# Row-wise self products on one core: new first blocks, shorter waits on GpSimd, and fifteen small loads behind the last store

## The chip, the core and the metric

The kernel runs on one core of a Trainium2 chip. The metric is the device time of one execution, in microseconds, as a median over runs. Products are made on VectorE (DVE), ScalarE (ACT) and GpSimd (POOL); SyncE (SP) issues the stores and GpSimd most of the loads; 16 DMA engines move the data. TensorE only counts the first stores.

## The reference

For each of 4096 rows of 256 floats, all products of two entries of the row with i <= j, in the order of the upper triangle:

```
dot = jnp.einsum('bi,bj->bij', inputs, inputs)      # inputs: (4096, 256) float32
iu, ju = jnp.triu_indices(256)
return dot[:, iu, ju]                               # (4096, 32896) float32
```

The input has 4.2 MB and the output 539 MB.

## The kernel before

The input lies in SBUF as one tile `x`: each of the 128 partitions holds 32 rows, in 16 groups of two (`REPEAT`), so one group is 256 rows of the output. The 32896 columns of a group are cut at multiples of 64 into three *pieces* (`PIECES`) of 10944, 10944 or 11008 columns. A piece of 128 x 2 rows fills one of two places, `o0` and `o1`, and leaves as one store of about 11 MB. Within a piece the work is a list of *runs* (`runs`): for one i, the products x[i] * x[j] for consecutive j. One VectorE or GpSimd instruction does a run for both rows of a group (two runs at once at some places), one ScalarE activation does a run for one row.

The loop (`all_pieces`) runs over `passes` = 8 times two groups, each time over `PASS` = 6 pieces. In it `tail` gives the last runs of a piece, up to a budget of 19.4 us by its cost function, to VectorE, and the others to GpSimd (`blocks`, with `ahead` false). VectorE reads one operand from `xv`, a copy of the current group in SBUF, and the other from `xp`, a copy in PSUM; GpSimd reads both from `xv`. `interleave` and `schedule` order the instructions so that one which writes one element into the next run's place is followed by that run a few instructions later, with a wait between them. Before a piece VectorE waits until the place's earlier store has landed (`free`) and passes that on through `go`, which GpSimd waits for (line 330). When GpSimd is done with a piece it waits for its own counter `g_own` and raises `g_done` (line 348). SP (`sync`) waits for `v_done` and `g_done` and issues the store of the piece.

The first two pieces (`ahead` true) are made differently. The first is cut at `FIRST` into six blocks that are stored one by one, so that the stores begin early; `split` divides the runs of a block between ScalarE (first runs) and VectorE (the rest), by cost functions in nanoseconds. In its first block VectorE reads both operands from `x`; then it copies `x` to `xp` in PSUM (line 232), takes GpSimd's `x_copied` (line 239) and goes on with `xv` and `xp`. In the second piece (`HELPED`) GpSimd does the last runs, up to 15 us, after `go`.

SP issues three loads at the start (`NEAR`; the first brings the first group), the rest of `x` comes from GpSimd: ten loads (`EARLY`, nine of which take every ninth partition, 14 each) with a small load, `mark`, between them, and further loads in the third turn of the loop (`LATE`). A `mark` brings two short runs of `MARK` floats to each of some partitions of a tile `marks` that nothing reads; the number of its partitions, with that of the loads, sets which DMA engines the next load uses. Right after the first load of these GpSimd waits for the first group and copies it to `xv` (lines 417 to 419).

At the end SP takes the counters of the loads and, last, `free` of both places (lines 427 to 431): the kernel ends when the last store has landed.

Of the kernel before, what the change touches and what calls it, by code (L numbers as in the profile page):

```python
# [8 lines left out]
F32 = mybir.dt.float32  # L9
# [3 lines left out]
P = 128  # L13
UNIT = 64
REPEAT = 2
# [9 lines left out]
COMB = 9  # L25
FORE, AFT = 5, 14
TENS, FIVES, SKIP = 100, 25, 2
MARK = 64
PLACES = 2
SETS = 5  # L30
PASS = 6
# [1 line left out]


BUDGET = 19.4
FIRST = [512, 1536, 3072, 5568, 9664]


def even_borders(lo: int, hi: int, pieces: int) -> list[int]:
# [67 lines left out]
    return sum(270 + 1.66 * REPEAT * n * m for (*_, n), m in vector_ops(block))  # L107


def split(block: list) -> int:  # L110

    def longer(k: int) -> float:
        scalar = sum(REPEAT * (184 + 0.837 * n) for *_, n in block[:k])
        return max(scalar, vector_time(block[k:]))

    return min(range(len(block) + 1), key=longer)


def tail(block: list, budget: float) -> int:
# [8 lines left out]
def kernel(  # L128
# [31 lines left out]
    edge = pool.tile([P, EDGE], F32, name="edge")  # L160
    places = [pool.tile([P, REPEAT, slot], F32, name=f"o{k}") for k in range(PLACES)]
    xt = pool.tile([P, passes, rounds * each], F32, name="x")
    xv = pool.tile([P, each + 1], F32, name="xv")
    marks = pool.tile([P, 2, 2 * MARK], F32, name="marks")

# [6 lines left out]
    free = [semaphore(f"free{k}") for k in range(PLACES)]  # L172
    head, v_done, a_done, go = (semaphore(s) for s in ("head", "v_done", "a_done", "go"))
    loaded = [semaphore(f"loaded{k}") for k in range(len(NEAR))]
    far, marked = semaphore("far"), semaphore("marked")
    teeth = P // COMB
    rest = P - COMB * teeth

# [9 lines left out]
    def blocks(p: int, ahead: bool):  # L188

        lo, hi = spans[p % PIECES]  # L190
        cuts = [lo, *(FIRST if ahead and p == 0 else []), hi]
        for a, b in zip(cuts, cuts[1:]):
            block = runs(d, a, b)
            if ahead:
                if p == HELPED:
                    block = block[: tail(block, HELP)]
                k = split(block)
                yield a - lo, b - lo, block[:k], block[k:], lo
            else:
                k = tail(block, BUDGET)  # L200
                yield a - lo, b - lo, block[k:], block[:k], lo
# [12 lines left out]
    def vector(h, pieces: range, ahead: bool, done: int = 0) -> int:  # L214
        for p in pieces:
            place, copied = places[p % PLACES], None
            if p % PIECES == 0:
                if not ahead:
                    take(nc.vector, x_read, 1)
                parts = blocks(p, ahead)  # L220
                if ahead:
                    _, _, _, block, lo = next(parts)
                    for i, j, at, length in block:
                        ins = nc.vector.tensor_tensor(  # L224
                            place[:, :, at - lo : at - lo + length],
                            window(x_of(h, 0)[:, j:], [[d, REPEAT], [1, 1], [1, length]]),
                            window(x_of(h, 0)[:, i:], [[d, REPEAT], [1, 1], [0, length]]),
                            ALU.mult,
                        )
                    ins.then_inc(v_done, 1)  # L230
                for to in (xp,) if ahead else (xv[:, :each], xp):
                    ins = nc.vector.tensor_copy(to, x_of(h, p // PIECES))  # L232
                    if done:
                        ins._wait_ge(v_own, done)
                    ins.then_inc(v_own, 1)
                    done += 1
                copied = done
                if ahead:
                    take(nc.vector, x_copied, 1)
                    nc.vector.wait_ge(v_own, copied).then_inc(go, 1)  # L240
                    copied = None
            else:
                parts = blocks(p, ahead)
            if not ahead:
                if use(p) < uses:
                    nc.vector.wait_ge(free[p % PLACES], 16 * use(p)).then_inc(go, 1)  # L246
                else:
                    take(nc.vector, free[p % PLACES], 16 * uses)
                    nc.vector.sem_inc(go, 1)  # L249
            for _, _, _, block, lo in parts:  # L250
                order = interleave(block)

                own = (p + 1) % PIECES == 0 or p == pieces[-1]
                waits = schedule(order)
                counted = {*waits.values(), *([len(order) - 1] if own else [])}
                number = {k: done + 1 + c for c, k in enumerate(sorted(counted))}
                for k, ((i, j, at, length), m, _) in enumerate(order):
                    at -= lo
                    ins = nc.vector.tensor_tensor(  # L259
                        place[:, :, at : at + m * length],  # L260
                        window(xv[:, j:], [[d, REPEAT], [1, m], [1, length]]),
                        window(xp[:, i:], [[d, REPEAT], [1, m], [0, length]]),
                        ALU.mult,
                    )
                    if copied:
                        ins._wait_ge(v_own, copied)
                        copied = None
                    elif k in waits:
                        ins._wait_ge(v_own, number[waits[k]])
                    if k in counted:  # L270
                        ins.then_inc(v_own, 1)
                done += len(counted)
                if own:
                    nc.vector.wait_ge(v_own, done).then_inc(v_done, 1)
                else:
                    ins.then_inc(v_done, 1)
        return done
# [45 lines left out]
    def gpsimd(h, pieces: range, ahead: bool):  # L323

        done = turns = 0
        for p in [HELPED] if ahead else pieces:
            place = places[p % PLACES]
            block, lo = helped(p) if ahead else next((block, lo) for _, _, block, _, lo in blocks(p, False))
            turns += 1
            nc.gpsimd.wait_ge(go, turns)  # L330
            order = interleave(block)
            waits = schedule(order)
            counted = {len(order) - 1, *waits.values()}
            number = {k: done + 1 + c for c, k in enumerate(sorted(counted))}
            for k, ((i, j, at, length), m, _) in enumerate(order):
                at -= lo
                ins = nc.gpsimd.tensor_tensor(  # L337
                    place[:, :, at : at + m * length],
                    window(xv[:, j:], [[d, REPEAT], [1, m], [1, length]]),
                    window(xv[:, i:], [[d, REPEAT], [1, m], [0, length]]),  # L340
                    ALU.mult,
                )
                if k in waits:
                    ins._wait_ge(g_own, number[waits[k]])
                if k in counted:
                    ins.then_inc(g_own, 1)
            done += len(counted)
            nc.gpsimd.wait_ge(g_own, done).then_inc(g_done, 1)  # L348
            if p in (BEGUN, HAD) and not ahead:
                late(h, p)  # L350
            if (p + 1) % PIECES == 0:
                nc.gpsimd.sem_inc(x_read, 1)
        if turns:
            nc.gpsimd.sem_inc(g_own, -done)
            nc.gpsimd.sem_inc(go, -turns)

    def sync():
        parts_done = done = joined = 0
        for turn in range(passes * PASS):
# [5 lines left out]
            for lo, hi, *_, base in parts:  # L365
                done += 1
                parts_done += ahead
                nc.sync.wait_ge(v_done, done)
                if ahead and p == HELPED:
                    nc.sync.wait_ge(g_done, joined)  # L370
                to = x_out[h, p // PIECES, :, :, base + lo : base + hi]
                store = nc.sync.dma_start(to, place[:, :, lo:hi])
                store._wait_ge(*((a_done, parts_done) if ahead else (g_done, joined)))
                store.then_inc(free[p % PLACES] if len(parts) == 1 else head, 16)
        for sem, count in ((v_done, done), (a_done, parts_done), (g_done, joined)):
            nc.sync.sem_inc(sem, -count)

# [27 lines left out]
        to, of = (window(ap[:, one * each :], dims) for ap in (flat, x_in))  # L405
        nc.sync.dma_start(to, of).then_inc(sem, 16)
    nc.vector.memset(edge, 0.0).then_inc(warm, 1)  # L407
    nc.vector.memset(xv[:, each:], 0.0)  # L408
    take(nc.scalar, warm, 1)
    nc.scalar.activation(edge[:, :1], edge[:, 1:2], AF.Copy, scale=edge[:, 2:3])  # L410
    for engine in (nc.vector, nc.scalar):
# [2 lines left out]
    for k in range(COMB + 1):  # L414
        load(EARLY, slice(k, k + COMB * (teeth - 1) + 1, COMB) if k < COMB else slice(P - rest, P))
        mark(FORE + rest * k, FORE + rest * k + (rest if k < COMB else AFT))
        if k == 0:
            nc.gpsimd.wait_ge(loaded[0], 16)
            nc.gpsimd.tensor_copy(xv[:, :each], x_of(0, 0)).then_inc(x_copied, 1)  # L419

    take(nc.tensor, head, 16 * (len(FIRST) + 1))
    nc.tensor.sem_inc(free[0], 16)
# [2 lines left out]
        all_pieces(engine, pieces_of)  # L425
    sync()
    take(nc.sync, x_read, 1)
    for sem in loaded:
        take(nc.sync, sem, 16)
    for k in range(PLACES):  # L430
# [28 lines left out]
```

## Time and profile before

| | |
|---|---|
| median of 3 runs | 1262.91 us (1262.59 to 1263.63) |
| profiled execution | 1263.23 us, its span 1261.4 us |
| DVE, ACT, POOL busy | 792.5, 27.3 and 804.4 us |
| stores | 53, of 0.5 to 11 MB, all issued by SP |
| first store issued, last store issued | 5.1 and 1228.6 us from the span's start |
| HBM read and written | 4.21 and 538.97 MB |

The span runs from the first to the last instruction of the core. The page counts instructions that compute as busy; issuing a DMA or waiting on a semaphore is not busy. The DMA row gives the mean busy share of the 16 DMA engines in 40 slices of the span; a letter q behind an engine's name stands for its queue of waits, counters and DMA issues.

### The profile page before, as it was taken

To read this page: it belongs to the slowest core of one execution; us is meant where nothing else is said; L and a number is where in the kernel's file an instruction comes from. 1 tells how busy PE (TensorE), PEld (TensorE's weight loads), DVE (VectorE), ACT (ScalarE), POOL (GpSimd) and SP (SyncE) were. 2 spreads that over 40 slices of the span, in tenths; PEclk is the share of its full clock that TensorE was granted. 3 is DMA by queue.
4 is the path that set the end of the run, shared out by engine and by line. 5 is a ranking of instruction groups with operands and counts; after the bars stand their busy time and mean duration, and the time that the engine had idled before them with its cause. 6 is when DMAs were issued, how large, how long until landed. Compare 5 with 4: busy or idle time off the path is not lost. (4 is left out here: it accounts for less than half of the span.)

```text
span 1261.4 us, 2976 instructions
## 1 busy us (share of the span) xinstructions
DVE 792.5 (63%) x1256; ACT 27.3 (2%) x74; POOL 804.4 (64%) x1133
## 2 busy tenths in 40 slices
DVE  8656747667474674766747666486655866468560
ACT  8000000000000000000000000000000000000000
POOL 8477665776566766577655775567656675576750
DMA  9999999999999999999999999999999999999998
GB/s 378 441 432 434 434 434 433 433 433 435 434 432 425 435 435 430 438 431 437 431 436 431 437 430 438 429 437 430 437 431 437 428 440 428 439 429 438 430 437 370
DMA packets 16408, 543.26 MB, mean 431 GB/s; under 512 B 1769, under 2 KB 1808, under 8 KB 3856
## 3 DMA queue, kind: packets, MB, share of 16 engines
q1 hardware_dynamic: 14976, 540.54, 99.2%
q0 software_dynamic: 1424, 2.65, 0.6%
q14 instruction: 8, 0.07, 0.0%
HBM read 4.21 MB, written 538.97 MB: 431 GB/s over the span
## 5 line engine op out<-in xcount | busy, mean ns | idle before, releaser
L337 POOL TENSOR_TENSOR o<-xv 128x52 f32<-128x52 f32 (+34 forms) x1103 | 788.5, 755 | 416.1 <-DVEq L246 282.4
L259 DVE TENSOR_TENSOR o<-xv,xp 128x260 f32<-128x260 f32 (+20 forms) x1221 | 773.8, 710 | 423.5 <-DMA out_dram<-o 301.6
L285 ACT ACTIVATE o<-x 128x253 f32<-128x253 f32 (+34 forms) x72 | 25.7, 451 | 1.0 <-DMA x<-in_r_inputs_dram 1.0
L232 DVE COPY xv<-x 128x512 f32 x15 | 6.4, 427 | 8.3 <-DVEq L180 8.3
L232 DVE COPY xp<-x 128x512 f32 (+1 forms) x16 | 11.1, 694 | 0.5
L309 POOL DMA_DIRECT2D x<-in_r_inputs_dram x13 | 7.7, 590 | 0.8 <-POOL o L337 0.8
L303 POOL DMA_DIRECT2D marks<-in_r_inputs_dram x12 | 7.0, 583 | 1.2 <-SPq L167 1.2
L224 DVE TENSOR_TENSOR o<-x 128x510 f32<-128x510 f32 (+1 forms) x2 | 1.2, 630 | 2.7 <-DMA x<-in_r_inputs_dram 2.7
L419 POOL COPY xv<-x 128x512 f32<-128x512 f32 x1 | 1.1, 1122 | 0.4 <-DMA x<-in_r_inputs_dram 0.4
L410 ACT ACT_TABLE_LOAD x1 | 1.3, 1283 | 1.2 <-ACTq L180 1.2
L407 DVE MEMSET edge<- 128x32 f32 x1 | 0.1, 85 | 1.0 <-SPq L167 1.0
L410 ACT ACTIVATE edge<-edge 128x1 f32<-128x1 f32 x1 | 0.3, 294 | 0.0
L446 POOL MEMSET const-float32-0.0<- 128x1 f32 x1 | 0.1, 98 | 0.2 <-issue 0.2
L446 POOL MEMSET const-bfloat16-1.0<- 128x1 bf16 x1 | 0.1, 101 | 0.0
L446 POOL MEMSET const-uint8-127<- 128x1 uint8 x1 | 0.1, 101 | 0.0
L446 POOL MEMSET const-float32-1.0<- 128x1 f32 x1 | 0.1, 98 | 0.0
L408 DVE MEMSET xv<- 128x1 f32 x1 | 0.1, 59 | 0.0
## 6 DMA issues: line engine op xcount, KB each, us to landing
out_dram<-o SPq DMA_DIRECT2D x31, 10944.0 KB, 33.5
out_dram<-o SPq DMA_DIRECT2D x16, 11008.0 KB, 31.4
out_dram<-o SPq DMA_DIRECT2D x1, 4096.0 KB, 16.1
out_dram<-o SPq DMA_DIRECT2D x1, 2496.0 KB, 11.9
out_dram<-o SPq DMA_DIRECT2D x1, 1536.0 KB, 8.8
out_dram<-o SPq DMA_DIRECT2D x1, 1280.0 KB, 17.2
x<-in_r_inputs_dram POOLq DMA_DIRECT2D x1, 1200.0 KB, 40.0
x<-in_r_inputs_dram SPq DMA_DIRECT2D x1, 1024.0 KB, 5.1
```

What stands on the lines that cost most here:

```text
L224: ins = nc.vector.tensor_tensor(place[:, :, at - lo : at - lo + length], window(x_of(h, 0)[:, j:], [[d, REPEAT], [1, 1], [1, length]]), wi ...
L232: ins = nc.vector.tensor_copy(to, x_of(h, p // PIECES))
L259: ins = nc.vector.tensor_tensor(place[:, :, at : at + m * length], window(xv[:, j:], [[d, REPEAT], [1, m], [1, length]]), window(xp[:, i:] ...
L285: nc.scalar.activation(places[p][:, r, at - lo : at - lo + length], xa[:, r * d + j : r * d + j + length], AF.Copy, scale=xa[:, r * d + i ...
L303: nc.gpsimd.dma_start(marks[lo:hi, :, :MARK], of).then_inc(marked, 16)
L309: nc.gpsimd.dma_start(to, of).then_inc(far, 16)
L337: ins = nc.gpsimd.tensor_tensor(place[:, :, at : at + m * length], window(xv[:, j:], [[d, REPEAT], [1, m], [1, length]]), window(xv[:, i:] ...
L407: nc.vector.memset(edge, 0.0).then_inc(warm, 1)
L408: nc.vector.memset(xv[:, each:], 0.0)
L410: nc.scalar.activation(edge[:, :1], edge[:, 1:2], AF.Copy, scale=edge[:, 2:3])
L419: nc.gpsimd.tensor_copy(xv[:, :each], x_of(0, 0)).then_inc(x_copied, 1)
L446: nc = _bacc.Bacc("TRN2", target_bir_lowering=False, num_devices=1)
```

## The change

- The first piece is cut at four columns instead of five: five blocks instead of six. In the first three VectorE reads both operands from `x`, without a copy; ahead of the fourth (`DIRECT`) it copies `x` to `xp`. `split` balances the engines over all blocks so far instead of each block alone, and counts that copy as 700 ns (`COPY`).
- GpSimd makes the copy to `xv` after all its first loads and marks instead of after the first load, together with the setting of the one element behind it, which VectorE did. VectorE waits for `x_copied` ahead of the second piece. In the second piece GpSimd no longer waits for `go`.
- In the loop GpSimd's wait for `go` is put on its first product, and `g_done` is raised by its last product, except in the last piece of a group, where it still waits for `g_own`.
- `mark` brings runs of 16 floats instead of 64.
- Behind the last store SP issues fifteen loads to a new tile `tiny`, which nothing reads: the k-th over k partitions, 2 k floats each (8 to 120 bytes per partition). SP takes their counter `probed` at the end, ahead of those of the other loads and of `free`.

```diff
@@ -25,7 +25,7 @@
 COMB = 9
 FORE, AFT = 5, 14
 TENS, FIVES, SKIP = 100, 25, 2
-MARK = 64
+MARK = 16
 PLACES = 2
 SETS = 5
 PASS = 6
@@ -33,7 +33,9 @@
 
 
 BUDGET = 19.4
-FIRST = [512, 1536, 3072, 5568, 9664]
+FIRST = [704, 1984, 3968, 6592]
+DIRECT = 3
+COPY = 700
 
 
 def even_borders(lo: int, hi: int, pieces: int) -> list[int]:
@@ -107,13 +109,19 @@
     return sum(270 + 1.66 * REPEAT * n * m for (*_, n), m in vector_ops(block))
 
 
-def split(block: list) -> int:
-
-    def longer(k: int) -> float:
-        scalar = sum(REPEAT * (184 + 0.837 * n) for *_, n in block[:k])
-        return max(scalar, vector_time(block[k:]))
-
-    return min(range(len(block) + 1), key=longer)
+def scalar_time(block: list) -> float:
+    return sum(REPEAT * (184 + 0.837 * n) for *_, n in block)
+
+
+def split(block: list, alone: bool, busy: list) -> int:
+
+    def ends(k: int) -> list:
+        vector = sum(vector_time([run]) for run in block[k:]) if alone else vector_time(block[k:])
+        return [busy[0] + scalar_time(block[:k]), busy[1] + vector]
+
+    k = min(range(len(block) + 1), key=lambda k: max(ends(k)))
+    busy[:] = ends(k)
+    return k
 
 
 def tail(block: list, budget: float) -> int:
@@ -160,6 +168,7 @@
     edge = pool.tile([P, EDGE], F32, name="edge")
     places = [pool.tile([P, REPEAT, slot], F32, name=f"o{k}") for k in range(PLACES)]
     xt = pool.tile([P, passes, rounds * each], F32, name="x")
+    tiny = pool.tile([P, 240], F32, name="tiny")
     xv = pool.tile([P, each + 1], F32, name="xv")
     marks = pool.tile([P, 2, 2 * MARK], F32, name="marks")
 
@@ -172,7 +181,7 @@
     free = [semaphore(f"free{k}") for k in range(PLACES)]
     head, v_done, a_done, go = (semaphore(s) for s in ("head", "v_done", "a_done", "go"))
     loaded = [semaphore(f"loaded{k}") for k in range(len(NEAR))]
-    far, marked = semaphore("far"), semaphore("marked")
+    far, marked, probed = (semaphore(s) for s in ("far", "marked", "probed"))
     teeth = P // COMB
     rest = P - COMB * teeth
 
@@ -188,13 +197,16 @@
     def blocks(p: int, ahead: bool):
 
         lo, hi = spans[p % PIECES]
-        cuts = [lo, *(FIRST if ahead and p == 0 else []), hi]
-        for a, b in zip(cuts, cuts[1:]):
+        alone = ahead and p == 0
+        cuts, busy = [lo, *(FIRST if alone else []), hi], [0, 0]
+        for c, (a, b) in enumerate(zip(cuts, cuts[1:])):
             block = runs(d, a, b)
+            if c == DIRECT:
+                busy[1] += COPY
             if ahead:
                 if p == HELPED:
                     block = block[: tail(block, HELP)]
-                k = split(block)
+                k = split(block, alone, busy)
                 yield a - lo, b - lo, block[:k], block[k:], lo
             else:
                 k = tail(block, BUDGET)
@@ -214,33 +226,36 @@
     def vector(h, pieces: range, ahead: bool, done: int = 0) -> int:
         for p in pieces:
             place, copied = places[p % PLACES], None
-            if p % PIECES == 0:
-                if not ahead:
-                    take(nc.vector, x_read, 1)
-                parts = blocks(p, ahead)
-                if ahead:
-                    _, _, _, block, lo = next(parts)
+            parts = blocks(p, ahead)
+            if ahead and p == 0:
+                for c, (_, _, _, block, lo) in enumerate(parts):
+                    if c == DIRECT:
+                        nc.vector.tensor_copy(xp, x_of(h, 0)).then_inc(v_own, 1)
+                        done += 1
+                        copied = done
                     for i, j, at, length in block:
                         ins = nc.vector.tensor_tensor(
                             place[:, :, at - lo : at - lo + length],
                             window(x_of(h, 0)[:, j:], [[d, REPEAT], [1, 1], [1, length]]),
-                            window(x_of(h, 0)[:, i:], [[d, REPEAT], [1, 1], [0, length]]),
+                            window(xp[:, i:] if c >= DIRECT else x_of(h, 0)[:, i:], [[d, REPEAT], [1, 1], [0, length]]),
                             ALU.mult,
                         )
+                        if copied:
+                            ins._wait_ge(v_own, copied)
+                            copied = None
                     ins.then_inc(v_done, 1)
-                for to in (xp,) if ahead else (xv[:, :each], xp):
+                continue
+            if ahead and p == HELPED:
+                take(nc.vector, x_copied, 1)
+            if not ahead and p % PIECES == 0:
+                take(nc.vector, x_read, 1)
+                for to in (xv[:, :each], xp):
                     ins = nc.vector.tensor_copy(to, x_of(h, p // PIECES))
                     if done:
                         ins._wait_ge(v_own, done)
                     ins.then_inc(v_own, 1)
                     done += 1
                 copied = done
-                if ahead:
-                    take(nc.vector, x_copied, 1)
-                    nc.vector.wait_ge(v_own, copied).then_inc(go, 1)
-                    copied = None
-            else:
-                parts = blocks(p, ahead)
             if not ahead:
                 if use(p) < uses:
                     nc.vector.wait_ge(free[p % PLACES], 16 * use(p)).then_inc(go, 1)
@@ -323,14 +338,19 @@
     def gpsimd(h, pieces: range, ahead: bool):
 
         done = turns = 0
+        if ahead:
+            nc.gpsimd.memset(xv[:, each:], 0.0).then_inc(g_own, 1)
+            nc.gpsimd.tensor_copy(xv[:, :each], x_of(0, 0)).then_inc(g_own, 1)
+            done += 2
+            nc.gpsimd.wait_ge(g_own, done).then_inc(x_copied, 1)
         for p in [HELPED] if ahead else pieces:
             place = places[p % PLACES]
             block, lo = helped(p) if ahead else next((block, lo) for _, _, block, _, lo in blocks(p, False))
-            turns += 1
-            nc.gpsimd.wait_ge(go, turns)
+            turns += not ahead
+            last = (p + 1) % PIECES == 0
             order = interleave(block)
             waits = schedule(order)
-            counted = {len(order) - 1, *waits.values()}
+            counted = {*waits.values(), *([len(order) - 1] if last else [])}
             number = {k: done + 1 + c for c, k in enumerate(sorted(counted))}
             for k, ((i, j, at, length), m, _) in enumerate(order):
                 at -= lo
@@ -340,18 +360,23 @@
                     window(xv[:, i:], [[d, REPEAT], [1, m], [0, length]]),
                     ALU.mult,
                 )
-                if k in waits:
+                if k == 0 and not ahead:
+                    ins._wait_ge(go, turns)
+                elif k in waits:
                     ins._wait_ge(g_own, number[waits[k]])
                 if k in counted:
                     ins.then_inc(g_own, 1)
             done += len(counted)
-            nc.gpsimd.wait_ge(g_own, done).then_inc(g_done, 1)
+            if last:
+                nc.gpsimd.wait_ge(g_own, done).then_inc(g_done, 1)
+            else:
+                ins.then_inc(g_done, 1)
             if p in (BEGUN, HAD) and not ahead:
                 late(h, p)
-            if (p + 1) % PIECES == 0:
+            if last:
                 nc.gpsimd.sem_inc(x_read, 1)
+        nc.gpsimd.sem_inc(g_own, -done)
         if turns:
-            nc.gpsimd.sem_inc(g_own, -done)
             nc.gpsimd.sem_inc(go, -turns)
 
     def sync():
@@ -372,6 +397,10 @@
                 store = nc.sync.dma_start(to, place[:, :, lo:hi])
                 store._wait_ge(*((a_done, parts_done) if ahead else (g_done, joined)))
                 store.then_inc(free[p % PLACES] if len(parts) == 1 else head, 16)
+        at = 0
+        for k in range(1, 16):
+            nc.sync.dma_start(tiny[:k, at : at + 2 * k], x_in[:k, : 2 * k]).then_inc(probed, 16)
+            at += 2 * k
         for sem, count in ((v_done, done), (a_done, parts_done), (g_done, joined)):
             nc.sync.sem_inc(sem, -count)
 
@@ -405,7 +434,6 @@
         to, of = (window(ap[:, one * each :], dims) for ap in (flat, x_in))
         nc.sync.dma_start(to, of).then_inc(sem, 16)
     nc.vector.memset(edge, 0.0).then_inc(warm, 1)
-    nc.vector.memset(xv[:, each:], 0.0)
     take(nc.scalar, warm, 1)
     nc.scalar.activation(edge[:, :1], edge[:, 1:2], AF.Copy, scale=edge[:, 2:3])
     for engine in (nc.vector, nc.scalar):
@@ -414,9 +442,7 @@
     for k in range(COMB + 1):
         load(EARLY, slice(k, k + COMB * (teeth - 1) + 1, COMB) if k < COMB else slice(P - rest, P))
         mark(FORE + rest * k, FORE + rest * k + (rest if k < COMB else AFT))
-        if k == 0:
-            nc.gpsimd.wait_ge(loaded[0], 16)
-            nc.gpsimd.tensor_copy(xv[:, :each], x_of(0, 0)).then_inc(x_copied, 1)
+    nc.gpsimd.wait_ge(loaded[0], 16)
 
     take(nc.tensor, head, 16 * (len(FIRST) + 1))
     nc.tensor.sem_inc(free[0], 16)
@@ -425,6 +451,7 @@
         all_pieces(engine, pieces_of)
     sync()
     take(nc.sync, x_read, 1)
+    take(nc.sync, probed, 16 * 15)
     for sem in loaded:
         take(nc.sync, sem, 16)
     for k in range(PLACES):
```

## The prediction

> **What bounds the kernel now.** I read the busy times first, then the 40 slices, the waits, SP's waits, and the two ends of the span by stages.
>
> From the page, the engines and the DMA rows:
>
> ```profile
> DVE 792.5 (63%) x1256; ACT 27.3 (2%) x74; POOL 804.4 (64%) x1133
> ...
> DMA  9999999999999999999999999999999999999998
> ...
> HBM read 4.21 MB, written 538.97 MB: 431 GB/s over the span
> ```
>
> No compute engine is busy for two thirds of the span, and the DMA engines are at nine tenths or more in every slice but the last. The waits and SP's waits say who follows whom:
>
> ```profile
> DVE o L259 <- DMA out_dram<-o: 301.6, 31, 15.9
> ...
> SPq L180 <- SPq L180: 30.9, 2, 25.9
> ```
>
> The first row is VectorE waiting for an earlier store to free its place; so products are ready before the transfers are. The second is the end: SP has issued the last store and sits 25.9 us in the take of its counter. The stages of the span, in microseconds, then busy time and count of DVE, ACT and POOL, PE's clock, DMA share and GB/s:
>
> ```profile
> 2.00:3.00 1.00, 0.00 (x0) 0.80 (x2) 1.00 (x3) 1.00 0.90 231
> 3.00:4.00 1.00, 0.21 (x1) 0.21 (x1) 0.64 (x2) 1.00 0.99 340
> 4.00:6.00 2.00, 1.85 (x4) 2.00 (x6) 2.00 (x3) 1.00 0.99 387
> 6.00:9.00 3.00, 3.00 (x8) 3.00 (x9) 3.00 (x7) 1.00 0.99 371
> 9.00:20.00 11.00, 11.00 (x19) 11.00 (x33) 10.90 (x15) 1.00 1.03 406
> ...
> 36.00:1220.00 1184.00, 757.07 (x1192) 0.00 (x0) 774.29 (x1083) 1.00 1.00 434
> ...
> 1256.00:1259.00 3.00, 0.00 (x0) 0.00 (x0) 0.00 (x0) 1.00 0.38 161
> 1259.00:1261.40 2.40, 0.00 (x0) 0.00 (x0) 0.00 (x0) 1.00 0.00 0
> ```
>
> Between 36 and 1220 us the transfers run at 434 GB/s without a hole, and nothing of the change acts on the transfers there. What can move lies in the first 20 us and the last 5. In the head, against 434 GB/s, the stages lose 0.47, 0.22, 0.22, 0.44 and 0.71 us: 2.05 us in all, much of it small packets and not idleness. At the end the share falls from full to nothing over three microseconds: the 16 DMA engines don't finish together. The trace's landings of the last store say it exactly: 16 increments between 1256.07 and 1260.28 us, the last of them 1.09 us behind the one before it. One DMA engine is late and alone, and it ends the kernel; SP's remaining instructions take 1.16 us after it. Following the landings of the 53 stores, that engine loses some 0.14 us to the others per store from 430 us on, because its 43 KB packets often take more than the usual 1618 ns, whatever the other engines do.
>
> **The profiled execution** took 1263.23 us: the span of 1261.44 and 1.79 around it. It lies 0.32 above the median of the runs, 1262.91. The sum below is a difference, so I add it to both. About 0.2% (2.5 us) is what a measurement of this kernel can tell from no change.
>
> **The head, part by part.** Stores there go from six (512, 1024, 1536, 2496, 4096, 1280 KB) to five (704, 1280, 1984, 2624, 4352). Would a DMA engine run dry? The kernel's own cost functions, which give 4.59 and 4.46 us for the first block where the trace has the store issued at 5.06, put the new blocks ready at about 4.9, 6.6, 9.4, 13.6 and 19.8 us, and SP issues each 0.2 to 0.6 later. Before, the six issues were at 5.06, 7.16, 9.08, 12.79, 18.35 and 20.35. The first store is no later: its second VectorE product grows from 2 to 2 x 193 elements (some 0.45 us), but VectorE's first product no longer shares the time with POOL's copy. Before the copy the engines still have the 1.5 MB of x loads in front of them until 6.8 us. After that they take at most 0.41 MB per us, so by 13.6 us they have moved less than 2.8 MB where 3.97 MB were handed over. No store arrives late, so what VectorE saves or adds (its 0.68 us copy to PSUM moves from behind the first block to before the fourth) lies under queued transfers. If that cover were gone the copy would cost its 0.68.
>
> What counts is DMA time alone. *One store less*: 16 packets less on each engine. A 2048-byte packet takes 84 ns and a 4096-byte one 159, so 9 ns are fixed, and 4 of those overlap the next packet: 16 x 5 ns = **-0.1 us**. *Marks*: 39 packets of 512 bytes at 27 ns become 128 bytes, by the same line 13.7 ns. If a dozen are on the late engine, 0.16 us; if none, nothing: **-0.1**, ends 0 and -0.2. *POOL's copy goes behind the loads*: POOL stood from 3.46 to 4.90 us at the wait and the copy, then issued the other load and mark pairs, 0.56 us each, until 15.0. Now it issues them 1.44 us earlier, and the copy with its memset (1.1 + 0.1) comes last; its helping products begin at about 14.9 instead of 15.1. Some 0.15 MB (1.3 loads of 112 KB) moves into time in which the rows above lose 0.2 us: **-0.1**, ends 0 and -0.3. VectorE now takes x_copied only ahead of the second piece, near 20 us, with the copy done by 15.
>
> **The loop.** The wait on `go` rides on POOL's first product, and g_done on its last one for two pieces of three. That takes some 0.1 us from POOL's path per piece, but a store waits behind the one before it: the issue-to-landing median of 33.5 us for 26 us of data is 7 us of queue. **0**, and if that queue were empty, 50 pieces x 0.1 = 5 us gain, which the full DMA rows exclude.
>
> **The tail: fifteen tiny loads.** SP issues them right after the last store at 1228.6; a store's issue takes it 0.37 to 0.39 us, a first load 0.39 to 0.46, so 15 take 5.5 to 7 us and are over by about 1236, 20 us before the last store's data is. Each then stands in the queue behind the last store on the engines it uses. On one engine a tiny load is one packet and one counter write. The trace has no load behind a store in one queue, so bounds. Upper row: the first packet of an x load took 602 ns instead of 84, one among stores 516 instead of 159, so 0.36 to 0.52 us of read latency shows when a read can't run ahead. Lower row: from the second x load to the third, at about 5.8 us, packets took 84 to 105 ns right behind the counter write, so nothing shows when it can. I take **+0.25** once, nearer the middle. Each load more costs the writes themselves: 9 ns the counter, 9 to 27 the data, starts 6 ns apart at the least, say 20 ns; between 0 and 15 of them on the late engine: 0 to 0.5, I take 8, **+0.15**. The counter lands 0.33 us after its write as a store's does, no addition. Last, SP's new take of `probed` stands ahead of the takes of three `loaded` and two `free`; the records have them 67 ns apart: 5 x 67 ns = **+0.3** if the probe lands last, 0 if the store still does. Tail: +0.7, ends 0 and +1.3.
>
> *A rule of the skill.* The Trainium skill, "DMA: Bandwidth & Descriptors", in "Why a DMA increments its semaphore by 16 and not by 1", says that a load over k partitions issued from SP runs on the lowest-numbered k (at most 16) engines; then engine 0 would get fifteen, engine 14 one and engine 15 none, and were the late engine the last, the tail would be 0. No row here numbers the engines. The same page, "Anatomy of one DMA", puts a fixed 2.0 us on any DMA, mostly the receipt of its last write; the row says 0.33 us from counter write to landing, and by the page's figure, paid once behind the last store, the tail would be an estimated 2.3 us.
>
> **Sum**: -0.1 - 0.1 - 0.1 + 0.25 + 0.15 + 0.3 = +0.4 us. 1262.91 + 0.4 = **1263.3** (profiled 1263.6).
>
> **The rivals.** *Slower: the tiny loads don't overlap.* Each is a round trip of its own on an engine. Price: a first read of 0.6 plus 0.33 to land is 0.93 us; the engine with fifteen ends at 15 x 0.93 = 14 us behind its store, and with the 1 to 4 us that the other engines have in hand and 0.3 of takes, the kernel is 10 to 13 us later: 1273 to 1276. It decides from about (1.1 + 2.5) / 15 = 0.24 us per load. For it: nothing in the trace has fifteen loads of one packet behind each other. A milder form of the same serialising: if SP's queue holds no more transfers than the three seen outstanding at once, a dozen are issued only when the last store lands: 12 x 0.4 + 0.9 + 0.3 = +6, 1269. Against both: counter writes and packets of successive loads and stores follow at 6 ns. I give the two 0.20.
>
> *Faster: the head loses less and the late engine is freed.* If the late engine no longer trailed, the second sets the end, 1.09 us earlier; with all 2.05 us that the head loses, -3.1 with nothing for the tail: 1259.8. For it: that engine's delay isn't explained by any row. Against: the loads of the head keep their bytes, and its slow packets come all through the run. 0.03.
>
> *The probe costs nothing*: the late engine has few or none of the loads and the others' are over within their 1.09 us. Then -0.3: 1262.6. It lies within the same 0.2%, and I count it there; the forecast with it has 0.77.
>
> **How the numbers follow.** The likeliest case spans -0.3 - 0.3 to +1.3, with 0.5 of the runs' own spread on either side: 1261.8 to 1264.7. Its 0.77 is less than what the range should hold, so it reaches on into the serial case to the price of 0.2 us per load, 1266.6. Faster 0.03, same 0.77, slower 0.20.
>
> **What would show it.** Right: 15 loads issued by about 1236 us; one more landing group behind the last store within 1 us of its latest increment; the DMA row unchanged, 434 GB/s in the middle; store issues at about 5.1, 6.8, 9.6, 14 and 20 us; POOL's helping products at 14.9. Wrong: tiny loads landing one by one hundreds of nanoseconds apart, their issues pushed past 1236, or a middle stage that isn't at 434.

## The result, and the profile after

The changed kernel takes 1266.12 us (median of 13 runs, 1265.62 to 1266.52), the kernel before 1263.34 in the same comparison (13 runs, 1262.59 to 1264.32). The ratio is 1.0019, 95% interval 1.0012 to 1.0027: 2.8 us by the medians, just over the 0.2% (2.5 us) that were called measurable, and clear of no change. The forecast was 1263.3 with a range of 1261.8 to 1266.6. The profiled execution took 1266.47 us, its span 1264.7.

The page of the changed kernel, the engines and the DMA rows:

```profile
DVE 792.5 (63%) x1257; ACT 27.8 (2%) x76; POOL 805.0 (64%) x1134
...
DMA  9999999999999999999999999999999999999997
...
HBM read 4.21 MB, written 538.97 MB: 429 GB/s over the span
```

Only the last slice differs. The stages of the changed kernel, in the columns used before:

```profile
2.00:3.00 1.00, 0.00 (x0) 0.80 (x2) 1.00 (x3) 1.00 0.76 205
3.00:4.00 1.00, 0.00 (x0) 0.00 (x0) 1.00 (x2) 1.00 0.98 348
4.00:6.00 2.00, 1.75 (x4) 1.75 (x6) 2.00 (x5) 1.00 1.00 394
6.00:9.00 3.00, 3.00 (x6) 3.00 (x10) 3.00 (x6) 1.00 1.04 387
9.00:20.00 11.00, 10.97 (x22) 11.00 (x31) 10.74 (x16) 1.00 1.02 401
...
36.00:1220.00 1184.00, 756.73 (x1191) 0.00 (x0) 774.54 (x1081) 1.00 1.00 433
...
1256.00:1259.00 3.00, 0.00 (x0) 0.00 (x0) 0.00 (x0) 1.00 0.48 193
1259.00:1261.00 2.00, 0.00 (x0) 0.00 (x0) 0.00 (x0) 1.00 0.02 1
1261.00:1263.00 2.00, 0.00 (x0) 0.00 (x0) 0.00 (x0) 1.00 0.00 0
1263.00:1264.70 1.70, 0.00 (x0) 0.00 (x0) 0.00 (x0) 1.00 0.00 0
```

Head and middle carry what they carried. At the end the rows show nothing from 1261 us on, and before the change from 1259; but they count a packet where it starts. By the packet records the last packet ends at 1260.78 us, 3.9 us before the end of the span; before the change it ended at 1259.83, 1.6 us before it. So the stretch at the end in which no DMA engine moves anything is 2.3 us longer. What SP does there, by its timeline and by its waits:

```profile
1229.30 0.37 SPq L397 DMA_DIRECT2D out_dram<-o  x1
1229.72 15.12 SPq L402 DMA_DIRECT2D tiny<-in_r_inputs_dram  x15
```

```profile
SPq L189 <- SPq L189: 18.1, 1, 18.1
```

It issues the tiny loads until 1244.8 us, and then sits 18.1 us in the take of `probed` (it waits for the counter and lowers it), where it sat in that of `free`. A DMA engine ends its part of a transfer with a counter write, a packet of 4 bytes in the records; that counter's *landing* is the moment at which the semaphore is recorded as raised. The landing records show what SP waits for. The last DMA engine's increments, in microseconds:

```
the last store      1261.161
the eleven loads    1261.349  1261.533  1261.717  1261.901  1262.085  1262.269
                    1262.453  1262.637  1262.821  1263.005  1263.189
SP passes probed    1263.205, then five takes, the last at 1263.537
```

The *packets* of these eleven loads and their counter writes are over in 0.16 us, between 1260.61 and 1260.78. Their *landings* come 184 ns apart, one behind the other.

### The profile page after: what moved, and what is told of

The parts are those of the page before. It is cut to its first block, busy times and chain, and to the rows that moved or that the text cites. A ratio compares the mean times of both kernels' runs of the same rounds, so it can differ in the third digit from the quotient of the medians.

```text
span 1264.7 us, 2963 instructions
## 1 busy us (share of the span) xinstructions
DVE 792.5 (63%) x1257; ACT 27.8 (2%) x76; POOL 805.0 (64%) x1134
## 5 line engine op out<-in xcount | busy, mean ns | idle before, releaser
L274 DVE TENSOR_TENSOR o<-xv,xp 128x356 f32<-128x356 f32 (+4 forms) x1196 | 759.7, 722 | 423.7 <-DMA out_dram<-o 302.1
L300 ACT ACTIVATE o<-x 128x198 f32<-128x198 f32 (+35 forms) x74 | 26.2, 460 | 1.4 <-DMA x<-in_r_inputs_dram 1.4
L253 DVE COPY xp<-x 128x512 f32 x15 | 10.4, 695 | 0.5
L237 DVE TENSOR_TENSOR o<-x,xp 128x470 f32<-128x470 f32 (+18 forms) x19 | 9.7, 590 | 0.0
L237 DVE TENSOR_TENSOR o<-x 128x510 f32<-128x510 f32 (+9 forms) x10 | 5.7, 648 | 3.1 <-DMA x<-in_r_inputs_dram 3.1
```

What stands on the lines that cost most here:

```text
L237: ins = nc.vector.tensor_tensor(place[:, :, at - lo : at - lo + length], window(x_of(h, 0)[:, j:], [[d, REPEAT], [1, 1], [1, length]]), wi ...
L274: ins = nc.vector.tensor_tensor(place[:, :, at : at + m * length], window(xv[:, j:], [[d, REPEAT], [1, m], [1, length]]), window(xp[:, i:] ...
L300: nc.scalar.activation(places[p][:, r, at - lo : at - lo + length], xa[:, r * d + j : r * d + j + length], AF.Copy, scale=xa[:, r * d + i ...
```

## The experiments

Two theories stood against each other. **A**: the counters of the loads land one behind the other on each DMA engine, some 184 ns each, eleven on the engine that ends the kernel: 2.02 us, and 0.33 for the five takes behind. **B**: the tail is as cheap as forecast, and the moved loads and new blocks cost the rest; the changed kernel's profile had the last store itself land at 1261.16 instead of 1260.28. All times are medians with the number of runs, beside `before` measured together with them (1263.80 for `no_probe`, `probe_only`, `one_load` and `two_engines`, 1263.64 for `sixteen_parts`, `own_counters`, `from_sbuf` and `take_last`; for the others it stands beside the time).

**Without the probe.** The changed kernel less these lines:

```diff
-        at = 0
-        for k in range(1, 16):
-            nc.sync.dma_start(tiny[:k, at : at + 2 * k], x_in[:k, : 2 * k]).then_inc(probed, 16)
-            at += 2 * k
...
-    take(nc.sync, probed, 16 * 15)
```

> The changed kernel without the fifteen loads and without the take of their counter. Theory A, that the loads' counters land one behind the other on each DMA engine (some 184 ns each, eleven on the engine that finishes last, 2.0 us, plus 0.33 us for the five takes behind that of probed): 1263.3 to 1264.0 us, 2.1 to 2.8 below the changed kernel. Rival B, that the earlier loads and new blocks at the head, or the other meeting of transfers when the later loads come at 375 to 430 us, make the kernel longer (its profile had the last store's landing 0.9 us later than before): 1264.0 to 1265.0. If the tail were as cheap as predicted (0.7 us): 1265.4.

1263.54 us (11 runs), ratio to before 0.9999 (0.9989 to 1.0008). Its stages at the end:

```profile
1256.00:1259.00 3.00, 0.00 (x0) 0.00 (x0) 0.00 (x0) 1.00 0.27 117
1259.00:1261.10 2.10, 0.00 (x0) 0.00 (x0) 0.00 (x0) 1.00 0.00 0
```

All of the change but the probe is worth nothing that can be measured, and B falls. The last store landed at 1259.99 here, and between 1260.08 and 1261.08 in the other kernels below with eleven or fifteen loads on the last engine. So of the 0.9 us by which it landed later in the changed kernel's profile than before, most is the spread from one profiled execution to the next.

**The probe alone**, on the kernel before (with marks of 16 floats):

```diff
-MARK = 64
+MARK = 16
...
+        at = 0
+        for k in range(1, 16):
+            nc.sync.dma_start(tiny[:k, at : at + 2 * k], x_in[:k, : 2 * k]).then_inc(probed, 16)
+            at += 2 * k
...
+    take(nc.sync, probed, 16 * 15)
```

> The kernel before, with marks of 16 floats (the new tile needs the space) and the fifteen loads with their take behind the last store; head and loop as before. Theory A: before plus 2.0 plus 0.33, 1265.5 to 1265.9 us, and in the profile eleven counter landings some 0.18 us apart on the last engine. Rival B: 1264.0 to 1264.5, since the probe would cost 0.7.

1266.31 us (11 runs), ratio 1.0020 (1.0011 to 1.0029): the whole loss, 0.4 above A's upper end. Its landings on the last engine are 184 ns apart again.

**One load instead of fifteen.**

```diff
-        for k in range(1, 16):
+        for k in (15,):
...
-    take(nc.sync, probed, 16 * 15)
+    take(nc.sync, probed, 16)
```

> The changed kernel with one tiny load only, over 15 partitions, in place of fifteen. Theory A: one counter more on the last engine, 0.18 plus 0.33 us, so 1.8 below the changed kernel, 1264.2 to 1264.5 us. Rival C, that it is a fixed latency paid once behind the last store (a round trip of 2 us): as the changed kernel, 1265.9 to 1266.3.

1263.87 us (11 runs), 0.3 below A's lower end of 1264.2 and far from C. In its profile the last store lands at 1260.111 and the load at 1260.299, 188 ns on. There is no fixed latency of microseconds behind the store; the tail grows with the number of loads.

**Fifteen loads on two engines.**

```diff
-            nc.sync.dma_start(tiny[:k, at : at + 2 * k], x_in[:k, : 2 * k]).then_inc(probed, 16)
+            nc.sync.dma_start(tiny[:2, at : at + 2 * k], x_in[:2, : 2 * k]).then_inc(probed, 16)
```

> The changed kernel with its fifteen loads all over 2 partitions, 30 descriptors in place of 120, so on two DMA engines by the pattern of the changed kernel's trace (a load over k partitions showed on k engines). Theory A: the two engines land fifteen counters, 2.7 us behind their last store, but they finish their stores 3 to 4 us before the last engine, so they are hidden and the time is that of the kernel without the loads within 0.4 us (the takes), 1263.5 to 1264.3. Rival D, that the number of loads in SP's queue or their issue counts, on whichever engines: as the changed kernel, 1266.1.

1263.45 us (11 runs): free. SP's waits show a second wait again where the changed kernel has one, and the issues took as long:

```profile
SPq L189 <- SPq L189: 15.9, 2, 14.9
```

```profile
L402 SPq DMA_DIRECT2D tiny<-in_r_inputs_dram x15: 279/1053/1063, 1229.2 to 1243.0; - x15
```

The last load lands at 1259.21, before the last store at 1260.49. Fifteen loads and their slow issue cost nothing where they are not on the engine that ends last. D falls.

**Fifteen on every engine, with one packet and with four.**

```diff
-            nc.sync.dma_start(tiny[:k, at : at + 2 * k], x_in[:k, : 2 * k]).then_inc(probed, 16)
+            nc.sync.dma_start(tiny[:16, at : at + 2 * k], x_in[:16, : 2 * k]).then_inc(probed, 16)
```

> The changed kernel with its fifteen loads all over 16 partitions, one packet of each on every DMA engine. Theory A: fifteen counters on the last engine instead of eleven, 4 x 0.184 = 0.74 us more than the changed kernel, 1266.7 to 1267.0 us. Rival C (a fixed latency once): 1266.1. It also shows whether SP's issue of 1.03 to 1.13 us per load, seen from the third load on, comes from loads over less than 16 engines: then it falls to the 0.37 us of a store.

(and with 64 in place of 16)

> The changed kernel with its fifteen loads all over 64 partitions: fifteen counters on each DMA engine as with 16 partitions, but four packets for each. Theory A, a fixed step per counter: steps of 0.18 us and the time of the run over 16 partitions, 1266.7 to 1267.0 us. Rival I, a step per small packet written: four times the steps, 15 x 0.55 = 8 us more, 1275.

1266.71 us (7 runs) and 1266.91 us (8 runs, `before` 1263.54 there). In both the landings on the last engine stay 184 ns apart; four packets to a counter don't change the step, so it belongs to the counter and not to the packet. (There is one counter for each load on each engine, so counter and load can't be told apart here.) The guess on SP's issues failed: each took longer, not 0.37 us, and with 64 partitions the last two took 4.1 and 6.5 us. The lines of the two kernels, shortest, median and longest in ns:

```profile
L402 SPq DMA_DIRECT2D tiny<-in_r_inputs_dram x15: 945/1161/1177, 1229.3 to 1245.9; - x15
```

```profile
L402 SPq DMA_DIRECT2D tiny<-in_r_inputs_dram x15: 1134/1321/6463, 1228.8 to 1250.5; - x15
```

**A counter of its own for each load.**

```diff
-    far, marked, probed = (semaphore(s) for s in ("far", "marked", "probed"))
+    far, marked = semaphore("far"), semaphore("marked")
+    probed = [semaphore(f"probed{k}") for k in range(15)]
...
-            nc.sync.dma_start(tiny[:k, at : at + 2 * k], x_in[:k, : 2 * k]).then_inc(probed, 16)
+            nc.sync.dma_start(tiny[:k, at : at + 2 * k], x_in[:k, : 2 * k]).then_inc(probed[k - 1], 16)
...
-    take(nc.sync, probed, 16 * 15)
+    for sem in probed:
+        take(nc.sync, sem, 16)
```

> The changed kernel with a semaphore of its own for each of the fifteen loads, taken one by one in order. Theory A (each DMA engine lands its counters one behind the other whatever semaphore they are for): as the changed kernel, 1265.8 to 1266.5 us, landings on the last engine still some 0.18 us apart. Rival E, that increments of one semaphore are what queues up: the landings come together and the time falls by about 1.8 us, to 1264.3.

1266.01 us (10 runs), steps of 183 to 195 ns on the last engine: the queue is the DMA engine's, not the semaphore's. E falls.

**From SBUF instead of HBM.**

```diff
-            nc.sync.dma_start(tiny[:k, at : at + 2 * k], x_in[:k, : 2 * k]).then_inc(probed, 16)
+            nc.sync.dma_start(tiny[:k, at : at + 2 * k], edge[:k, : 2 * k]).then_inc(probed, 16)
```

> The changed kernel with the fifteen loads taken from a small SBUF tile instead of the input in HBM. Theory A, if the step of 0.18 us is the round trip of the counter and of the data written: as the changed kernel, 1265.8 to 1266.5 us, steps of 0.18 us. Rival F, that the step is the read from HBM: steps well below 0.18 us and the time towards that without the loads, 1264.0 to 1264.5.

1265.67 us (10 runs), steps of 184 ns. The read from HBM isn't the step; F falls.

**The take of the probe last.**

```diff
     for k in range(PLACES):
         take(nc.sync, free[k], 16 * uses)
+    take(nc.sync, probed, 16 * 15)
```

> The changed kernel with SP's take of probed moved behind those of the loads and of free, so that one take and not six follows the last landing. If the takes cost what the records say (67 ns each): 0.33 us less than the changed kernel, 1265.8 us; if they are hidden: no difference.

1265.62 us (11 runs). From the last landing to the end of the span it is 1.16 us, as before the change; in the changed kernel 1.49. The 0.33 us of the takes are real.

**Can the last engine be relieved?** It ends 1.3 us behind the next in the kernel without the probe. Two kernels built on that one give it less to load, and a third only issues the later loads earlier:

```diff
-NEAR = [(0, 1, 1), (3, 7, 2), (12, 13, 1)]
+NEAR = [(0, 1, 1), (3, 7, 2)]
...
-LATE = (9, 13, 3)
+LATE = (9, 16, 7)
...
-        dims = [[(two - one) * each, 2], [1, units * each]]
+        dims = [[(two - one) * each, 2 if two - one > units else 1], [1, units * each]]
...
-        with nc.gpsimd.If(h == WHEN):
+        with nc.gpsimd.If(h == (WHEN - 1 if p == BEGUN else WHEN)):
```

> The kernel without the probe, with one of SP's three first loads (group 12, 128 partitions over all 16 DMA engines, 8 packets of 2 KB each) left out and its data brought by the later loads of GpSimd, which spare the engine that finishes last; those are issued one pass of the loop earlier and waited for where they were. Theory G, that one engine's own sum of packets sets the end: that engine has 8 x 80 ns = 0.64 us less, others 0.1 more to 0.26 less, so 0.6 us below the kernel without the probe, 1262.9 us; its last landing 0.8 us behind the second instead of 1.3. Rival H, that the late engine ends late whatever it carries (its packets stretch to fill): no difference, 1263.5.

1266.37 us (11 runs, `before` 1263.54): 2.8 longer. With `NEAR = [(0, 1, 1), (3, 5, 2)]` and `LATE = (7, 16, 9)`:

> The same with groups 7 and 8 too: SP's first loads bring three groups instead of six, 1.9 us less on the late engine; the ten engines that carry most of the later loads gain 0.35 to 0.6 us. Theory G: the late engine and the others end together, 1.0 us below the kernel without the probe, 1262.5 us. Rival H: 1263.5.

1268.59 us (5 runs): 5.1 longer. With the last of the four edits alone:

> The kernel without the probe, with its later loads (unchanged in what they bring) issued one pass of the loop earlier and waited for where they were; SP's first loads as they were. It tells apart why the two kernels with fewer first loads were 2.8 and 5.1 us longer than before instead of 0.6 and 1.0 shorter. If issuing the later loads earlier is the cause: 1266 us, with the last DMA engine some 4 us behind all others at the end. If leaving out SP's first loads is: 1263.5, as the kernel without the probe.

1264.48 us (10 runs, `before` 1264.06, ratio 1.0005, 0.9995 to 1.0014): between the two expectations, and no more above `before` than can be measured, though the last engine landed 2.5 us behind the next in its profile instead of 1.3. So most of the loss comes with the first loads that SP no longer makes, or with the larger later loads that replace them; these two weren't told apart. Both theories, G and H, missed. A part is seen in the head, here of the kernel without the probe and then of the one with nine groups left for later:

```profile
4.00:6.00 2.00, 2.00 (x4) 2.00 (x7) 2.00 (x5) 1.00 1.00 391
6.00:9.00 3.00, 3.00 (x7) 3.00 (x10) 3.00 (x6) 1.00 1.04 384
```

```profile
4.00:6.00 2.00, 2.00 (x5) 2.00 (x7) 2.00 (x5) 1.00 0.67 229
6.00:9.00 3.00, 3.00 (x7) 3.00 (x10) 3.00 (x6) 1.00 0.96 289
```

The difference, at 434 GB/s, is 0.75 + 0.66 = 1.4 us of transfers not made: SP's first loads had filled that time. The rest stays open. In both kernels the other engines' landings of the last store stand within 0.3 us of each other, all but one at most, and the last engine some 4 us behind them. That would fit the others having waited for it, which no run here shows. Why it lagged more with less to load wasn't settled. No kernel of the study beats the one before by more than can be measured.

## Why the prediction was right, and where it was wrong

The time fell into the range, but not into its likeliest case, which ended at 1264.7: +2.8 us measured, +0.4 forecast. It lies in the part that the range took from the serial rival, up to 0.2 us per load, and two of the three signs of being wrong appeared: the tiny loads landed one by one, though 184 ns and not hundreds apart, and their issues ran past 1236 us. That the range held was partly luck. The engine that ends last carries eleven of the loads; with fifteen on it the same step gave 1266.71 and 1266.91 us, beyond 1266.6. By the prediction's steps:

- **The bound.** Right: 433 GB/s in the middle, nothing else of the change shows.
- **The head and the loop**, -0.3. Without the probe the time is 0.3 below before, not distinguishable from zero. Store issues stood at 5.11, 6.84, 9.64, 13.84 and 19.94 us in that kernel, for some 5.1, 6.8, 9.6, 14 and 20 expected (in the changed kernel's profile 0.4 later, because its first products began 0.4 later); GpSimd's products began at 14.52 instead of 14.9, because its copy took 0.62 us at its new place and not 1.12.
- **The engine that ends last decides.** Right, and sharper than forecast: fifteen loads on two other engines cost nothing. The number of loads on it was taken as 8 and is 11.
- **The takes**, +0.3: 0.33.
- **Read latency**, +0.25: wrong; one load lands 188 ns behind the store, no more than a step, so nothing of the read shows.
- **Each load, 20 ns.** This is the step that failed. The sum priced a load by its packets (measured: about 14 ns each with its counter write) and said of the counter that it "lands 0.33 us after its write as a store's does, no addition". A store's counters are 26 us apart on an engine, so their landing delay overlaps the next store; the loads' counters are written some 14 ns apart and land 184 ns apart. Eleven of them are 2.02 us where 0.15 stood. With it the sum is -0.3 + 2.02 + 0.33 = +2.05, with the head at zero 2.35; measured 2.8 and, for the probe alone, 2.5.
- **A term that the sum didn't have**, +0.2. With the probe the last store itself ended later on the last engine, by one profile of each kernel. Its sixteen packets took 26.17 us in the changed kernel (26.16 to 26.18 in the others with eleven loads there) and 26.03 without the probe; in `two_engines`, with none there, they took 26.11, so not all of this comes from loads on that engine. And its counter landed 0.55 us after its write instead of 0.47. The 0.33 us of the prediction is that of the other engines, 0.32 to 0.39 before the change; the last one had 0.46 there. With these 0.2 us the probe is worth 2.6, as far as runs can tell.
- **The serial rival** was right that the loads land one by one, with a step five times too long (0.93 us), because it repeated the read with every load; the packets of all eleven were over in 0.16 us. Its milder form, a full queue at SP, didn't occur: all fifteen were issued by 1244.8 us. Its own point of decision, 0.24 us per load on the engine with fifteen, compares with 0.184 on the one with eleven, and its "counter writes follow at 6 ns" spoke of writes where landings count.
- **SP's issues**, 5.5 to 7 us: 15.1. Loads cost 1.03 to 1.13 us each from the third on. They were still over 16 us before the last store landed, and `two_engines`, with issues as long, lost nothing.

The skill's rules: "Why a DMA increments its semaphore by 16 and not by 1" (the Trainium skill, "DMA: Bandwidth & Descriptors") says that a load that SP issues over k partitions, k up to 16, runs on the lowest-numbered k engines. The records agree in form: behind the last store one engine carries fifteen tiny packets, one fourteen, and so on to one with none, each with the largest loads. The engine with eleven, the fifth in that order, ends last (store packets over at 1260.62; the next, with thirteen, at 1259.33). The fixed 2.0 us of "Anatomy of one DMA" on the same page is given there for DMAs that GpSimd issues, and SP issued these loads. It didn't appear behind the store: a single load cost 0.33 us by the medians, 1263.87 against 1263.54.

A sum of the steps seen, 1263.54 + 0.33 + 0.184 n with n counters on the last engine, gives 1264.05, 1265.89 and 1266.63 for n = 1, 11 and 15; measured 1263.87, 1265.67 to 1266.31 (with all six takes), and 1266.71 and 1266.91. The medians of `before` alone lie between 1263.34 and 1264.06 from one comparison to another, so a closer agreement can't be asked.

## What to carry to other kernels

Price small DMAs at the end of a kernel by their landings, not their packets: here each counter on the DMA engine that ended last took 184 ns of its own, and the count on that engine is what mattered. Look at the 16 landings of the last store: loads on an engine that ends early were free, as long as their landings were over before the last engine's. And a transfer that runs while nothing else could is free where it is: in `late_nine`, loads moved from the head to later left 1.4 us of the head unused.

## What the runs showed of the hardware

- Counters of successive small loads into SBUF landed 184 ns apart on the DMA engine that ended last, whatever the semaphore (own ones: 183 to 195), the source (HBM or SBUF: 184) and the packets for each (one or four: 184). On engines that ended early it was less: 163 and 175 on the first two with sixteen partitions, 170 and 174 with two engines alone. What sets the step stays open, and whether counters of stores have it wasn't tried.
- SP's issue of these small loads took 1.03 to 1.13 us each in the changed kernel, against 0.37 us for an 11 MB store; the first took 0.36 and the second 0.25. Two partitions instead of k gave the same, 16 gave 1.16 and 64 gave 1.32. What sets it wasn't tried further.
- One DMA engine falls behind the others in the later part of the run and ends 1.3 us behind the next. Without the probe, between 440 and 1200 us, some 330 of 7500 store packets are longer than the usual time, 4.1 us together; that is about what this engine loses there, but the packets weren't traced to it one by one.
